# Attention with seven of seven block products: 49 of 64 in passes over 1024 queries

## The chip, the cores and the metric

The kernel runs on one core of a Trainium2 chip, in fp32. The core has TensorE (PE in the profile; PEld are its weight loads), VectorE (DVE), ScalarE (ACT), GpSimd (POOL) and SyncE (SP, which here issues DMAs), and 16 DMA engines. The metric is the device time of the whole program in microseconds. Three runs of the kernel before took 3640.42, 3641.31 and 3642.59 us; the median is 3641.31.

## The reference

The input has two images of 512 channels and 64 x 64 pixels. Two layers are added to it one after the other, each on a group-normalised copy. Layer 0 is a deformable convolution; the change leaves it alone. Layer 1 is attention over the 4096 pixels of an image, an output projection, a batch norm over both images and a relu:

```python
px = jnp.transpose(x.reshape(B, C, N), (0, 2, 1))
q = jnp.tanh(px @ Wq.T)            # 64 wide
k = jnp.tanh(px @ Wk.T)
v = px @ Wv.T
scores = jnp.einsum('bip,bjp,p->bij', q, k, align_w)
attn = jax.nn.softmax(scores, axis=2)
content = px + attn @ v
content = content @ Wfc.T + bfc
out = g * (c - mean) * jax.lax.rsqrt(var + BN_EPS) + b
return jax.nn.relu(out)
```

Scores are bounded by the sum of the absolute values of `align_w`, since the tanh is between -1 and 1. So no maximum is subtracted, and the sum of the exponentials divides at the end. Queries, keys and their product with `align_w` are 64 wide; values are 512 wide, so the product of the exponentials with the values is the large one: 4096 x 4096 x 512 for each image.

## The kernel before

**Shape of the program.** Layer 0 (lines up to 1236) leaves the sum of the input and its own output in DRAM (`x1_d`), [channel, pixel], in eight chunks of 512 pixels for each image. Then comes the attention, which has two stages for each image, and at the end the batch norm over both images. The order of the instructions in this part is the order of the code (`manual_schedule`); each engine runs its own queue in that order and waits for others through semaphores.

**Values.** Wv and Wfc have been multiplied beforehand (`wc_d`), so the attention's value product gives the output projection at once. For each of four groups of 1024 pixels, `pk` (L1439) makes keys and queries with a tanh; then `values` (L1371 to L1400) makes values for four pairs of 128-pixel tiles. The product of each pair is itself made of seven block products in place of eight (a Strassen form of Winograd's kind): seven products of two matmuls into PSUM, one ACT copy (L1388) and eleven DVE operations (L1389 to L1399), and the result is stored to DRAM as the seven block combinations that the next stage wants (L1400). The sums of the pixels' blocks that the seven products need come from `sum_pixels` (L1279 to L1282), on DVE for the first group and on POOL for the others.

**Query blocks.** For each of eight blocks of 512 queries the kernel runs over 16 key pairs (256 keys) and two more steps with the output weights `w7`, which project the residual. In `produce` (two pairs ahead) PE makes the scores of a pair (L1345), ACT takes the exponential (L1349), and DVE forms the query side's block sums (L1352 to L1355) and adds to the total (L1362). Then PE multiplies with the values, which SP loads two pairs ahead. The matrix product is cut in 2 x 2 x 2 blocks, and seven block products take the place of eight. Six run side by side in the six PSUM banks (L1500), two matmuls each; the seventh runs in a pass of its own after the others (L1543) with the sums `t3` kept in SBUF and the seventh combination of the values loaded again. That makes 18 x 14 = 252 matmuls of 128x256 for each block. Near the end of the block PE adds the total over partitions and spreads it (`pr`, L1471), DVE scales the residual `xq` with it (L1472 to L1478) and takes the reciprocal (L1480). ACT and DVE evacuate the six banks (L1521 to L1526) while PE is in the seventh pass; `finish_chunk` adds the seventh product's part in the next block. Results of image 0 go to DRAM, those of image 1 stay in SBUF.

**Tail.** When both images are done, the batch statistics are made; for every chunk ACT applies scale, shift and relu, DVE adds the residual, and SP stores. Image 0's results and residuals are loaded back for it.

**Guard.** The attention runs on this fast path always. Behind it the core compares the sum of |align_w|, divided by `SCORE_MAX` (40, L527), with one, and two other bounds with their limits; only where one is passed does a general path run as well. For these inputs the sum of |align_w| is 3.83.

Of the kernel before, what the change touches and what calls it, by code (L numbers as in the profile page):

```python
# [2 lines left out]

# [14 lines left out]
P = 128  # L18
# [508 lines left out]
SCORE_MAX = 40.0  # L527
# [43 lines left out]
def window_path(ctx: ExitStack, tc: tile.TileContext, t_in: dict, out: bass.AP, far: bass.AP, sums: bass.AP):  # L571
# [8 lines left out]
    c0_d = dram.tile([NCH, P, KB, CH], F32, name="wc0")  # L580
    wc_d = dram.tile([P, KB, C], F32, name="wvfc")
    v_d = [[dram.tile([P, 7, C // 2], F32, name=f"wv{n}_{k}") for k in range(S // P // 2)] for n in range(NB)]
# [653 lines left out]
    with ExitStack() as l1, tc.manual_schedule():  # L1236
        cp = l1.enter_context(tc.tile_pool(name="w1c", bufs=NCH, reuse_waits="tile"))
        bnp = l1.enter_context(tc.tile_pool(name="w1bnp", bufs=1))
        bst = bnp.tile([P, KB, NB * NCH, 6], F32, name="bst")
        last, res = [], []  # L1240
        HC = C // 2
        HQ = CH // 2
        NPAIR = S // P // 2

        with ExitStack() as at, ExitStack() as inner:
            aw = at.enter_context(tc.tile_pool(name="w1w", bufs=1))
            wk = at.enter_context(tc.tile_pool(name="w1work", bufs=2))
            iw = l1.enter_context(tc.tile_pool(name="w1in", bufs=1, side="right", reuse_waits="tile"))
            vw = inner.enter_context(tc.tile_pool(name="w1v", bufs=3, side="right"))
            vv = inner.enter_context(tc.tile_pool(name="w1vv", bufs=3, side="right"))  # L1250
            ps = at.enter_context(tc.tile_pool(name="w1ps", bufs=1, space=PSUM))

            def bank(i, name):
                return ps.tile([P, CH], F32, tag=f"A{i}", name=name)

            class Bank:


                def tile(self, shape, dtype, tag, name):
                    return ps.tile(shape, dtype, tag="A5", name=name)  # L1260

            pixels = {}
            ones = iw.tile([P, P], F32, name="ones_k")
            nc.vector.memset(ones, 1.0)

            def chunk(n, ch, queue):
                t = cp.tile([P, KB, CH], F32, tag="c", name="xt")
                queue.dma_start(t, x1_d[n][ch])
                return t

            def load_pixels(n, i):

                pair = [chunk(n, 2 * i + h, nc.scalar if n or i == 0 else nc.sync) for h in range(2)]
                return pair, [cp.tile([P, 2, 2, CH], F32, tag="c", name=name) for name in ("xsa", "xsb")]

            def sum_pixels(engine, pair, sums):

                (a1, a2), (sa, sb) = [x.rearrange("p (j r) q -> p j r q", j=2) for x in pair], sums
                engine.tensor_add(sa[:, 0], a2[:, 0], a2[:, 1])  # L1279
                engine.tensor_sub(sa[:, 1], sa[:, 0], a1[:, 0])  # L1280
                engine.tensor_sub(sb[:, 0], a1[:, 0], a2[:, 0])
                engine.tensor_sub(sb[:, 1], a1[:, 1], sa[:, 1])  # L1282

            def value_output():
                t = wk.tile([P, KB, C], F32, tag="x", name="wc", bufs=1)
                nc.sync.dma_start(t, wc_d)
                return t

            def sum_value_output(wc):

                t = wk.tile([P, 2, 4, HC], F32, tag="tx", name="wcs", bufs=1)
                b = wc.rearrange("p (j r) (l c) -> p j r l c", j=2, l=2)
                nc.vector.tensor_sub(t[:, :, 0, :], b[:, 0, :, 1, :], b[:, 0, :, 0, :])
                nc.vector.tensor_sub(t[:, :, 1, :], b[:, 1, :, 1, :], t[:, :, 0, :])
                nc.vector.tensor_sub(t[:, :, 2, :], b[:, 1, :, 1, :], b[:, 0, :, 1, :])
                nc.vector.tensor_sub(t[:, :, 3, :], t[:, :, 1, :], b[:, 1, :, 0, :])
                return t

            def normalize(t, sc, bi):
                for kb in range(KB):  # L1300
                    nc.scalar.activation(
                        t[:, kb, :], t[:, kb, :], AF.Identity, bias=bi[:, kb : kb + 1], scale=sc[:, kb : kb + 1]
                    )

            pixels[0] = load_pixels(0, 0)
            wc = value_output()
            pixels[1] = load_pixels(0, 1)
# [11 lines left out]
            w7 = aw.tile([P, 2, 7, HC], F32, name="w7")  # L1319
            bfc = load("L1_conv_bfc", [P, KB], None, aw)  # L1320
            gamma = load("L1_conv_gamma", [P, KB], None, bnp)
            beta = load("L1_conv_beta", [P, KB], None, bnp)
            for x in pixels[0][0]:
                normalize(x, *norms[0])
            sum_pixels(nc.vector, *pixels[0])
            wcs = sum_value_output(wc)

            kq = iw.tile([P, NCH, CH], F32, name="kq")
            qs, tots, made, vs, v7s = {}, {}, {}, {}, {}

            def queries(qb):

                rows = slice(DQ * (1 - qb % 2), DQ * (2 - qb % 2))
                nc.vector.tensor_scalar(kq[rows, qb, :], kq[rows, qb, :], al[rows], None, ALU.mult)
                q = vw.tile([P, CH], F32, name="q", bufs=2)
                for h in range(2):
                    nc.vector.tensor_copy(q[h * DQ : (h + 1) * DQ, :], kq[rows, qb, :])
                qs[qb] = q

            def produce(qb, kp):  # L1340

                pS = ps.tile([P, 2, CH], F32, tag="st", name="pS")
                for h in range(2):
                    c0, r = (kp % 4) * P, slice(h * DQ, (h + 1) * DQ)
                    nc.tensor.matmul(  # L1345
                        pS[:, h, :], kq[r, 2 * (kp // 4) + h, c0 : c0 + P], qs[qb][r, :], start=True, stop=True
                    )
                e = vw.tile([P, 4, HQ], F32, name="e")
                nc.scalar.activation(e.rearrange("p a q -> p (a q)"), pS.rearrange("p h q -> p (h q)"), AF.Exp)  # L1349
                tt = vw.tile([P, 3, HQ], F32, name="tt")  # L1350
                t3 = wk.tile([P, HQ], F32, name="t3", bufs=NPAIR + 2)
                nc.vector.tensor_sub(t3, e[:, 3, :], e[:, 1, :])  # L1352
                nc.vector.tensor_add(tt[:, 0, :], t3, e[:, 0, :])
                nc.vector.tensor_sub(tt[:, 2, :], tt[:, 0, :], e[:, 2, :])
                nc.vector.tensor_sub(tt[:, 1, :], e[:, 1, :], e[:, 0, :])  # L1355
                e2 = e.rearrange("p (h a) q -> p h (a q)", h=2)
                if kp == 0:
                    tots[qb] = vw.tile([P, CH], F32, name="tot", bufs=2)
                    nc.vector.tensor_add(tots[qb], e2[:, 0, :], e2[:, 1, :])
                else:  # L1360
                    for h in range(2):
                        nc.vector.tensor_add(tots[qb], tots[qb], e2[:, h, :])  # L1362
                made[qb, kp] = e, tt, t3

            def operands(b, tt):
                return (b(0), b(2), tt[:, 0, :], tt[:, 1, :], b(3), tt[:, 2, :])
# [305 lines left out]
```

## Time and profile before

The profiled execution has a span of 3638.9 us; the median of the timed runs is 2.4 us above it. The attention layer takes the last 2423 us.

| stretch of the span (us) | what runs | length | PE busy | DVE busy | DMA GB/s |
|---|---|---|---|---|---|
| 1216.2 to 1351.9 | values, image 0 | 135.7 | 131.1 | 103.6 | 173 |
| 1351.9 to 2386.2 | eight query blocks, image 0 | 1034.3 | 1034.3 | 522.5 | 134 |
| 2386.2 to 2516.7 | values, image 1 | 130.5 | 129.0 | 102.4 | 154 |
| 2516.7 to 3552.5 | eight query blocks, image 1 | 1035.8 | 1034.7 | 518.7 | 132 |
| 3552.5 to 3638.9 | batch norm, relu, stores | 86.4 | 0.6 | 43.9 | 373 |

A line of the windows gives a stretch, its length, and for each engine the busy time with the number of instructions, in the order PE, PEld, DVE, ACT, POOL; behind them the TensorE clock that was granted (1.00 is full), the share of time in which the DMA engines were busy, and GB/s. Each fp32 matmul is two instructions for PE. A line of a timeline gives start, duration, engine, line, operation, out<-in, shape and count; in brackets is how long the engine had been idle and who released it. A line of the groups gives busy time and mean ns of one behind the bar.

### The profile page before, as it was taken

What the parts mean: (1) busy time and instruction counts of PE and PEld (TensorE: products, weight loads), DVE (VectorE), ACT (ScalarE), POOL (GpSimd) and SP (SyncE); (2) the same over time, 40 slices, a digit from 0 to 9 for tenths busy, and PEclk for the clock granted to TensorE, in tenths of its full rate; (3) what the DMA queues carried; (4) which work ended last, traced back from release to release, by engine and by line L of the source; (5) the groups of instructions that cost most, each with busy time, mean ns of one, the idle gap of its engine ahead of it and who ended that gap; (6) DMA issues with size and microseconds to landing.
All of it is one profiled execution on the core that took longest, in us unless ns stands there. A gap on an engine that the chain in (4) does not pass through costs nothing.

```text
span 3638.9 us, 38933 instructions
## 1 busy us (share of the span) xinstructions
PE 3408.9 (94%) x15155; PEld 2428.8 (67%) x15155; DVE 2358.5 (65%) x3549; ACT 1306.8 (36%) x1693; POOL 284.7 (8%) x190
## 2 busy tenths in 40 slices
PE   5789999999998999999999999999999999999990
PEld 2355555555555677777777777777777777777770
DVE  8899999999996674554555455476455545545544
ACT  2577778878876321111211111121111111111115
POOL 1121121121120110000000000031000000000000
PEclk9899999999999999999999999999999999999995
DMA  6334334334323444333433433444333343333359
GB/s 213 98 114 139 125 94 127 119 94 128 114 84 111 169 169 152 125 125 126 142 124 113 156 124 102 143 182 176 125 130 113 104 153 111 113 132 124 113 186 376
DMA packets 173941, 497.31 MB, mean 137 GB/s; under 512 B 21520, under 2 KB 55056, under 8 KB 164272
## 3 DMA queue, kind: packets, MB, share of 16 engines
q1 hardware_dynamic: 165360, 460.09, 37.4%
q10 hardware_dynamic: 8352, 34.61, 2.6%
q8 instruction: 121, 1.98, 0.2%
q14 instruction: 76, 0.62, 0.0%
q0 software_dynamic: 32, 0.00, 0.0%
HBM read 403.34 MB, written 91.29 MB: 136 GB/s over the span
## 4 chain that ended last, share of the span: by engine, by line
PE 77%; DVE 15%; DMA 3%; ACT 2%; issue 1%; POOL 1%; SPq 0%; ACTq 0%; DVEq 0%; POOLq 0%
PE acc L1500 42%; DVE conv L814 10%; PE pS L1345 7%; PE p L1543 6%; PE py L998 6%; PE pq L783 5%; PE pa L978 5%; PE pv L1385 3%; PE pk L1439 1%; PE p_mean L830 1%; DMA early<-in_x 1%; DVE o L876 1%; DMA in_w<-in_L_conv_in_w 1%; DMA out<-ct 0%; DVE v L1399 0%
## 5 line engine op out<-in xcount | busy, mean ns | idle before, releaser
L1500 PE MATMUL acc<-e,v 128*128 128x256 f32 x3072 | 768.2, 386 | 0.0
L1349 ACT ACTIVATE e<-pS 128x1024 f32<-128x1024 f32 x256 | 262.2, 1024 | 1386.3 <-PE pS L1345 1317.9
L1500 PE MATMUL acc<-tt,v 128*128 128x256 f32 x3072 | 748.2, 380 | 0.2 <-DVE v L1396 0.2
L1500 PEld LDWEIGHTS acc<-e,v 128*128 128x128 f32 x3072 | 566.5, 190 | 233.2 <-issue 165.4
L1500 PEld LDWEIGHTS acc<-tt,v 128*128 128x128 f32 x3072 | 582.4, 190 | 91.0 <-issue 10.6
L1352 DVE TENSOR_TENSOR t<-e 128x256 f32<-128x256 f32 x256 | 108.9, 425 | 761.0 <-ACT e L1349 761.0
L814 DVE SCALAR_TENSOR_TENSOR conv<-xn,L_conv_dw_w_sb,conv 128x504 f32<-128x504 f32 (+1 forms) x512 | 409.4, 808 | 37.6 <-ACT conv L808 23.8
L1362 DVE TENSOR_TENSOR tot<-tot,e 128x512 f32<-128x512 f32 x480 | 330.3, 688 | 8.3
L1345 PE MATMUL pS<-q,kq 64*128 64x512 f32 x1024 | 289.0, 641 | 0.0
L978 PEld LDWEIGHTS pa<-bt,patch 96*128 96x128 f32 x2048 | 249.6, 196 | 57.0 <-issue 33.5
L978 PE MATMUL pa<-bt,patch 96*128 96x128 f32 x2048 | 253.6, 281 | 7.1 <-ACT bt L964 5.5
L964 ACT COPY bt<-pb 96x1024 f32<-96x1024 f32 x124 | 234.6, 2007 | 57.6 <-PE pb L959 55.3
L783 PE MATMUL pq<-in_w,xn 128*128 128x512 f32 x512 | 240.4, 613 | 6.6 <-DVE o L876 4.5
L998 PE MATMUL py<-dT,L_conv_out_w_sb 128*128 128x512 f32 x512 | 236.1, 605 | 4.8 <-ACT dT L989 4.8
L1543 PE MATMUL p<-t,v 128*128 128x256 f32 x1024 | 231.4, 382 | 1.1 <-DMA v<-wv 1.1
L1543 PEld LDWEIGHTS p<-t,v 128*128 128x128 f32 x1024 | 192.1, 190 | 47.8 <-issue 21.2
L871 PE MATMUL po<-om_w_pg,feat 128*128 128x432 f32 x512 | 203.7, 543 | 2.5 <-ACT feat L854 2.5
L989 ACT COPY dT<-pa 32x256 f32<-32x256 f32 x496 | 180.0, 363 | 65.7 <-PE pa L978 56.3
L998 PEld LDWEIGHTS py<-dT,L_conv_out_w_sb 128*128 128x128 f32 x512 | 97.5, 194 | 123.2 <-issue 112.6
L783 PEld LDWEIGHTS pq<-in_w,xn 128*128 128x128 f32 x512 | 95.3, 197 | 114.5 <-issue 98.7
L871 PEld LDWEIGHTS po<-om_w_pg,feat 128*128 128x128 f32 x512 | 93.7, 192 | 94.5 <-issue 89.2
L1345 PEld LDWEIGHTS pS<-q,kq 64*128 64x128 f32 x1024 | 77.1, 184 | 84.9 <-issue 84.9
(210 smaller groups left out, 3713.2 us busy)
## 6 DMA issues: line engine op xcount, KB each, us to landing
v<-wv SPq DMA_DIRECT2D x252, 768.0 KB
patch<-xt SPq DMA_DIRECT2D x256, 192.0 KB
v<-wv SPq DMA_DIRECT2D x256, 128.0 KB
wv<-v SPq DMA_DIRECT2D x32, 896.0 KB
xt<-xj SPq DMA_DIRECT2D x128, 128.0 KB
res<-in_x SPq DMA_DIRECT2D x64, 256.0 KB
wx<-res SPq DMA_DIRECT2D x64, 256.0 KB
xq<-wx SPq DMA_DIRECT2D x16, 1024.0 KB
```

The lines of the kernel that those rows point to most:

```text
L783: nc.tensor.matmul(pq, xn[:, kb, 1 + 2 * t : 3 + 2 * t, :].rearrange("p r c -> p (r c)"), in_w[:, kb, :], start=(kb == 0), stop=(kb == KB ...
L814: nc.vector.scalar_tensor_tensor(dst, src, wt, dst, ALU.mult, ALU.add)
L871: nc.tensor.matmul(po[:, : 3 * GP], f[:, kb, t * P : (t + 1) * P], om_w[:, kb].rearrange("p a k g -> p (a k g)"), start=(kb == 0), stop=(k ...
L964: copy(bt[:SN].rearrange("s g q d -> s d (g q)")[:, d0 : d0 + 4, :], pb[:SN])
L978: nc.tensor.matmul(pa[:, p], xp[:SN, p, cb * P : (cb + 1) * P], bt[:SN, 4 * cb : 4 * cb + 4, PX * s + p, :], start=True, stop=True,)
L989: copy(dst, src)
L998: nc.tensor.matmul(py, out_w[:, kb, cb * P : (cb + 1) * P], dT[:, kb, :], start=(kb == 0), stop=(kb == KB - 1))
L1345: nc.tensor.matmul(pS[:, h, :], kq[r, 2 * (kp // 4) + h, c0 : c0 + P], qs[qb][r, :], start=True, stop=True)
L1349: nc.scalar.activation(e.rearrange("p a q -> p (a q)"), pS.rearrange("p h q -> p (h q)"), AF.Exp)
L1362: nc.vector.tensor_add(tots[qb], tots[qb], e2[:, h, :])
L1500: nc.tensor.matmul(acc[j][:, cb * HQ : (cb + 1) * HQ], v[:, j, cb * P : (cb + 1) * P], ops[j], start=(kp + cb == 0), stop=(kp + cb == NPAI ...
L1543: nc.tensor.matmul(p7[:, cb * HQ : (cb + 1) * HQ], v7[:, cb * P : (cb + 1) * P], t3, start=(k + cb == 0), stop=(k + cb == NPAIR + 2),)
```

## The change

The product of the exponentials with the values is cut in 4 x 4 x 4 blocks, 64 of them, and the seven-of-eight form is used at both levels, so that 49 products remain. The outer level is run as seven passes, one after the other, over all keys; the inner level is run inside each slot of a pass.

- A chunk has 1024 queries (two of the old blocks). Its 63 slots are seven passes of nine: eight groups of 512 keys and one group for the output weights. A slot is seven matmuls of 128x256 (L1478 of the new file), so a chunk has 441. They add up in two PSUM tiles `accx` and `accy`, from a pool of three.
- The scores are made once for each chunk, 32 pairs in 32 events with slots given by the table `EVENTS`: 'e0' and 'e2' mostly in slots that belong to the chunk before, 'e3' in slots 5 to 12, 'e1' in slots 13 to 20. The exponentials of a whole chunk stay in SBUF. `settle`, one event later, turns them into the outer level's combinations in place: a total and a transform for e0 and e2, a transform for e3; for e1 also a second row made of e0, e1 and e3 and the total of the chunk's second half.
- The inner sums of a slot (`inner_sums`, L1457 and L1458) are made by DVE four slots ahead (`LEAD`), in five buffers. The values of a slot are loaded by SP three slots ahead (448 KB).
- `spread_total`, the sum over partitions of a total on PE (L1434), stands in slot 5 for the first half's total and in slot 22 for the second's, ahead of the slot's products; ACT copies it and `scale_residual` uses it. The total's last adds (`total`, L1428 and L1430) stand in slots 4 and 21. The reciprocals stand in slots 7 and 25.
- At the end of a pass `first_copy` and `collect` evacuate the two tiles, and the passes' results are added to four output pieces in turn.
- In the values stage each pair of tiles still takes seven products of two matmuls, but into PSUM tiles of the same pool of three; the evacuation is one ACT copy and five DVE operations (L1639 to L1644), and `forms` (L1332 to L1345) makes the two levels' combinations on DVE for each pair of pairs and stores them, 7 x 448 KB. Twelve score events of the image's first chunk are also in this stage. The output weights go through `forms` too, in image 0. Queries go through DRAM (`q_d`).
- All large tiles come from one ring of 36 pieces of 4 KB per partition (`w1ring`), so that a tile waits until the piece 36 tiles before it is done with.
- Results go to DRAM except for the last chunk's. The tail's loads begin at slot 47 of the last chunk, in pieces of 512 KB.
- `SCORE_MAX` goes from 40 to 6.

```diff
-SCORE_MAX = 40.0
+NG = S // P // 4
+SLOTS = 7 * (NG + 1)
+LEAD = 4
+SCORE_MAX = 6.0
...
-                            for cb in range(2):
-                                nc.tensor.matmul(
-                                    acc[j][:, cb * HQ : (cb + 1) * HQ], v[:, j, cb * P : (cb + 1) * P], ops[j],
-                                    start=(kp + cb == 0), stop=(kp + cb == NPAIR + 2),
-                                )
...
+        ring = l1.enter_context(tc.tile_pool(name="w1ring", bufs=36, reuse_waits="tile"))
...
+            def forms(raw, store):
+
+                for j in (0, 3, 1, 5):
+                    nc.vector.tensor_add(raw[j][:, 1, :], raw[j][:, 1, :], raw[j][:, 3, :])
+                yield
+
+                def finish(j):
+                    t = raw.pop(j)
+                    nc.vector.tensor_sub(t[:, 4, :], t[:, 0, :], t[:, 1, :])
+                    nc.vector.tensor_add(t[:, 5:7, :], t[:, 4, :].unsqueeze(1).to_broadcast([P, 2, P]), t[:, 2:4, :])
+                    nc.sync.dma_start(store[j], t[:, :7, :])
+
+                def combine(j, a, b):
+                    raw[j] = piece("vform", (P, 8, P))
+                    nc.vector.tensor_sub(raw[j][:, :4, :], raw[a][:, :4, :], raw[b][:, :4, :])
...
+            def transform(t):
+                x = blocks(t)
+                nc.vector.tensor_sub(x[:, 1], x[:, 1], x[:, 0])
...
+            def second_row(c, g):
+                t0, t1 = c.e["e0", g], c.e["e1", g]
+                nc.vector.tensor_sub(t0, t1, t0)
+                nc.vector.tensor_add(t1, t1, c.e["e3", g])
+                if g < NG:
+                    add_total(c, 1, t1)
+
+            def settle(c, key, g):
+
+                e = c.e[key, g]
+                if key in ("e0", "e2"):
+                    add_total(c, 0, e)
+                transform(e)
+                if key == "e1":
+                    second_row(c, g)
+
+            def total(c, qh):
+                t = c.tot[qh]
+                nc.vector.tensor_add(t[:, 1, :], t[:, 1, :], t[:, 0, :])
+                if qh:
+                    nc.vector.tensor_add(t[:, 1, HQ:], t[:, 1, HQ:], t[:, 0, :HQ])
+
+            def spread_total(c, qh):
+                p = pair_bank("pr")[:, 0, :]
+                nc.tensor.matmul(p, ones, c.tot.pop(qh)[:, 1, :], start=True, stop=True)
+                nc.scalar.copy(rin[:, qh, :], p)
...
+            def inner_sums(c, p, g):
+                x = blocks(c.e[ORDER[p][0], g])
+                t = wk.tile([P, 3, HQ], F32, name="tt", bufs=LEAD + 1)
+                nc.vector.tensor_sub(t[:, 0], x[:, 1], x[:, 3])
+                nc.vector.tensor_add(t[:, 1:3], t[:, 0].unsqueeze(1).to_broadcast([P, 2, HQ]), x[:, 0:3:2])
+                return t
...
+            EVENTS = {}
+            for g, l in enumerate((-14, -13, -11, -10, -9, -7, -6, -5)):
+                EVENTS.setdefault(l, []).append(("e0", g))
+            for g in range(NG):
+                EVENTS.setdefault(g - 4, []).append(("e2", g))
+                EVENTS.setdefault(5 + g, []).append(("e3", g))
+                EVENTS.setdefault(13 + g, []).append(("e1", g))
...
+                def slot(self, s):
+                    k, l = divmod(s, SLOTS)
+                    c = self.chunks[k]
+                    nxt = self.chunks[k + 1] if k + 1 < NCH // 2 else None
+                    self.fetch(s + 3)
+                    if l % (NG + 1) == 0 and self.ends:
+                        next(self.ends[-1], None)
+                    self.before(l, c)
...
+                    self.at(l, c, s)
+                    if l + LEAD not in (8, 26):
+                        self.sums(s + LEAD)
+                    if l in (4, 21):
+                        total(c, int(l > 4))
+                    p, g = divmod(l, NG + 1)
+                    products(c, p, g, self.v.pop(s), self.t.pop(s))
```

## The prediction

> **What bounds the kernel now.** I read the page's busy shares, the chain of waits, and then a table of windows, because the change touches only the attention layer, the last two thirds of the span.
>
> ```profile
> PE 3408.9 (94%) x15155; PEld 2428.8 (67%) x15155; DVE 2358.5 (65%) x3549; ACT 1306.8 (36%) x1693; POOL 284.7 (8%) x190
> ...
> PE 77%; DVE 15%; DMA 3%; ACT 2%; issue 1%; POOL 1%; SPq 0%; ACTq 0%; DVEq 0%; POOLq 0%
> ```
>
> PE carries most of the chain. The windows cut the attention layer into values of image 0, its eight query blocks, the same two for image 1, and the tail:
>
> ```profile
> core 0: us, PE busy (x) PEld busy (x) DVE busy (x) ACT busy (x) POOL busy (x), PEclk, DMA share, GB/s
> 1216.20:1351.90 135.70, 131.14 (x528) 99.20 (x529) 103.64 (x211) 35.01 (x57) 29.50 (x12) 0.99 0.45 173
> 1351.90:2386.20 1034.30, 1034.28 (x4549) 796.52 (x4550) 522.46 (x920) 171.80 (x190) 5.17 (x3) 1.00 0.40 134
> 2386.20:2516.70 130.50, 128.97 (x526) 97.53 (x524) 102.44 (x198) 29.33 (x50) 34.65 (x14) 1.00 0.40 154
> 2516.70:3552.50 1035.80, 1034.67 (x4548) 796.16 (x4548) 518.68 (x920) 167.43 (x183) 0.00 (x0) 1.00 0.38 132
> 3552.50:3638.90 86.40, 0.56 (x4) 0.16 (x3) 43.91 (x37) 45.73 (x65) 0.50 (x2) 0.52 0.95 373
> ```
>
> In the two long windows PE is never idle and its clock is full; DVE is half used (522 of 1034). In the values windows DVE stands at 104 of 136 and 102 of 131, much nearer. The tail is DMA at 0.95 of its engines. So PE work removed from the query blocks is worth its full time only while DVE keeps up, and work added to DVE in the values stage has little room.
>
> **Prices.** PE, from the timeline of one query block: twelve products of 128x256 follow each other in 2.59 us (row below: 2.75 with the drain of the last, next row starting 2.59 later), two instructions for each fp32 product, so 0.4317 us per product. A key pair's period is 6.43 us for 12 products; the remaining 1.25 is its score pair. DVE durations come from the rows:
>
> ```profile
> 1584.40 2.75 PE L1500 MATMUL acc<-tx,w 128*128 128x256 f32 x12
> 1586.99 1.24 PE L1500 MATMUL acc<-xq,w 128*128 128x256 f32 x5
> ```
> ```profile
> L1362 DVE TENSOR_TENSOR tot<-tot,e 128x512 f32<-128x512 f32 x480 | 330.3, 688 | 8.3
> L1352 DVE TENSOR_TENSOR t<-e 128x256 f32<-128x256 f32 x256 | 108.9, 425 | 761.0 <-ACT e L1349 761.0
> L1480 DVE RECIPROCAL rin<-pr 128x512 f32<-128x512 f32 x16 | 53.6, 3350 | 0.0
> ```
> ```profile
> 1216.77 1.21 DVE L1279 TENSOR_TENSOR xsa<-xt 128x1024 f32<-128x1024 f32 x1
> 1218.02 1.23 DVE L1280 TENSOR_TENSOR xsa<-xsa,xt 128x1024 f32<-128x1024 f32 x1
> ```
>
> So DVE pays 0.42, 0.69 and 1.22 us for 256, 512 and 1024 columns; dependent neighbours are spaced 0.47 and 1.25, independent ones 0.34, 0.61 and 1.14.
>
> **PE in the query blocks.** One block of before, from a window of its own:
>
> ```profile
> 1565.38:1695.12 129.74, 129.74 (x571) 99.63 (x571) 65.91 (x117) 21.01 (x23) 0.00 (x0) 1.00 0.39 130
> ```
>
> Two blocks (1024 queries) take 2 x 129.7 = 259.5 us: 504 products, 32 score pairs, two sums over partitions (0.86 each). After, one chunk has 63 slots of seven products: 441 x 0.4317 = 190.4, 32 score pairs 40.0, two sums 1.7; together 232.1, which is 27.4 less. The first twelve score pairs of each image (eight of e0, four of e2) come before its first slot, so 12 x 1.25 = 15 us of PE move into the values stage. Undisturbed, an image's attention would be 4 x 192.1 + 116 x 1.25 = 913 plus about 2 at its end, against 1034: minus 119.
>
> **DVE in the query blocks, and the stall.** Counted in the new program's order, one chunk gives DVE 107 operations of 256 columns, 86 of 512, 74 of 1024, two copies, eight bn_stats and two reciprocals: 44.9 + 59.3 + 90.3 + 1.4 + 5.5 + 6.7 = 208 us, against 2 x 65.9 = 132 now. That is 90% of PE's 232, so the mean fits; the question is where it bunches. It does in slots 13 to 21, where the scores called e1 arrive. Each is settled (L1417) with a transform (256), two operations of the second row (1024) and a total (1024): 0.47 + 1.25 + 1.25 + 1.14 = 4.1, and the slot's inner sums (256 and 512) make it 5.2 us. PE needs seven products and a score pair, 4.27. DVE starts about 2.4 us late (score to exp to DVE, as in the trace: 1.23 to the exp, 1.02 in it). Slot by slot it ends at 7.05 in slot 14, 22.6 in 17, 30.4 in 18 (which also evacuates the pass that has ended, 2.6), 36.7 and 43.1 in 19 and 20 (each with an add of a pass, 1.14), and 49.5 in 21 with the total's last adds. PE, unhindered, stands at slot 22 after 8 x 4.27 + 3.02 = 37.2. There its next instruction is the sum over partitions of that total (L1434), and all products of slot 22 are queued behind it. So PE waits about **12.3 us in each of eight chunks**. Bounds: 9, if independent operations keep a pitch of 0.34 and 0.61 throughout; 16, if the ring's pieces, which the last three e1 exps get only when PE has done with them (about 1.1 each), add to it. I take the middle walk, because its operations do depend on each other.
>
> After the wait PE starts at a lower clock. The trace shows this once in the values stage, where DVE shut out by POOL let PE idle 2.79 us:
>
> ```profile
> 1239.86 2.59 POOL L1279 TENSOR_TENSOR xsa<-xt 128x1024 f32<-128x1024 f32 x1 [107.60 <-ACT xt L1301]
> ...
> 1242.65 2.57 DVE L1398 TENSOR_TENSOR v<-v,u 128x256 f32<-128x256 f32 x1
> ...
> 1248.09 1.26 PE L1385 MATMUL pv<-wc,xsb 128*128 128x256 f32 x4 [2.79 <-DVE v L1389]
> ...
> 1249.14 1.91 PE L1385 MATMUL pv<-wcs,xsb 128*128 128x256 f32 x4
> ```
>
> Four products took 1.91 where they take 1.03; some 1.5 us was lost. I add 1.5 per stall (0 to 3). The page "TensorE: Matmul & The Clock Gate", section "What's actually happening", halves the clock only after an idle window of about 3.4 us; the row did so after 2.79. By the page the loss could be up to 3.4 us of half speed, 1.7 lost, so 1.6 us more over eight stalls, which changes nothing.
>
> Other waits on PE (slot 5's first sum, the pass boundaries with three accumulator tiles) come to at most 0.3 us each by the same walk, and the two reciprocals stand where PE has work for four slots; cost zero while the inner sums keep their lead of four slots (otherwise 3.35 each). One image's attention is then 913 + 4 x 13.8 + 2 = 970: **64 less than now, twice**.
>
> **Values stage.** PE: 16 tiles, 96.7; keys and queries 27.5; twelve score pairs 15: 139. DVE: 16 evacuations of 2.5 (three of 256, two of 512), 40; block sums (L1332), per pair of tiles four of 512, seven of 256 and eleven of 128 columns, the last not in the trace: between half a 256 operation and a whole one, taken as 0.29 from the line through 0.42 and 0.69: 8.6 to 9, times 8 = 69; twelve settles of 1.64, 20; first sums 4. Three blocks of POOL sums lie beside it: the rows above show a 256 operation with both inputs in SBUF at 2.5 us while POOL works, and one such block costs DVE about 6.4 us, so 19. DVE begins about 10 us into the stage. That is 162 to 164 us. The page "SBUF — State Buffer", section "Who interferes with whom", says the same of DVE operations with two SBUF inputs, and would let the block sums, all of that kind, wait as often as they meet a POOL operation; it speaks against this change, whose DVE work there is mostly such. If each POOL operation met one, the price would be 12 x 2.1 = 25 in place of 19. Then the first load of v stands on SP's queue behind the last store of block sums, which DVE ends; its landing costs 3 to 4. Image 1: 166 against 130.5, **plus 36**. Image 0 also forms the output weights' blocks, 8.6 more, and the second normalisation: 178 against 135.7, **plus 42**. Bounds for the two: plus 40 in all if DVE's part overlaps PE better (PE's 139 plus start and load) and plus 120 if POOL costs double.
>
> **Tail.** From slot 47 of the last chunk prefetches are issued. Some 14 MB of them and 7.3 MB of v must pass in 48 us, 441 GB/s, where the tail shows 373: PE waits for v some 5 (0 to 10). Behind PE's end the remaining bytes take about 89 against 86.4. **Plus 8** (0 to 12).
>
> **Sum.** -128 + 78 + 8 = -42 on the profiled span of 3638.9, so 3597 less a little; that execution lies 2.4 below the median 3641.3, which goes back on. I predict **3597 us** (3638.9 - 44 + 2.4).
>
> **Rivals.**
> *DVE catches up and the total is ready* (chance 0.10). The inner pitch of 0.34/0.61 in the rows speaks for it, the dependence of each settle's operations against. Without the stall: 3597 - 8 x 13.8 = 3487.
> *The e1 slots take longer, slower than before* (0.25). The total comes later by each e1 exp's wait for a ring piece: if all eight wait 1.1 us and DVE waits with them, a stall grows by 8.8, 70 us in all: 3667. The gain is gone from 5.5 us more per chunk (44 / 8), that is 0.6 us in each of nine slots. For it: 36 pieces hold 32 score tiles of a chunk and much else. Against: only three of eight exps wait in the order that I followed.
> *The change doesn't do what it says* (0.05): if the guard on scores sent these inputs down the general path, or the stall and the values stage took just the 219 us of products back. The sum of the absolute align weights, which bounds a score, is 3.83 here, under 6 as under 40, so only the second remains: 3641.
>
> **How the numbers follow.** The likeliest (0.60) is 3597, with its own range 3550 to 3635 from the stall's 9 to 16 and the stage's bounds. To leave out no more than 2 in 10 the range goes up to the slower rival, 3667, and down half way to the faster, 3530. About 0.2%, 7 us, is what a measurement of this kernel can tell. Faster 0.70 (the likeliest, less its upper edge, and the faster rival), same 0.05, slower 0.25.
>
> **What would show it.** In the changed kernel's waits: PE before the sum at L1434, released by DVE's total (L1428 or L1430), eight times about 12 us with the clock below full behind it. In windows: a values stage of 166 to 178 with DVE above 90% and PE waiting for it; chunks of about 246; 3528 products at two instructions each and 0.216 us. The prediction is wrong if the stall at L1434 is under 5 us or over 18, if PE waits for exps or for v in every slot, or if DVE's operations of 1024 columns take more than 1.25.

## The result and the profile after

The changed kernel takes 3677.22 us (median of four runs, 3674.86 to 3680.62) against 3640.86 us of the kernel before, measured beside it. The ratio is 1.0102, 95% interval 1.0088 to 1.0116: slower by one per cent, where 3597 us and faster had been forecast. The profiled execution has a span of 3673.1 us, 4.1 below the median.

The page's busy shares and chain of the changed kernel:

```profile
PE 3239.0 (88%) x14147; PEld 2261.1 (62%) x14147; DVE 2969.6 (81%) x4107; ACT 1362.9 (37%) x1802; POOL 272.5 (7%) x186
...
PE 63%; DVE 27%; DMA 4%; ACT 3%; issue 1%; POOL 1%; SPq 0%; ACTq 0%; DVEq 0%; POOLq 0%
```

PE lost 170 us of work and DVE won 611, and DVE's share of the chain went from 15% to 27%. The windows, cut at the same places of the program as before (columns as there):

```profile
1216.20:1436.40 220.20, 156.50 (x570) 108.03 (x569) 162.27 (x334) 61.24 (x89) 28.54 (x12) 0.84 0.52 196
1436.40:2413.90 977.50, 925.89 (x4004) 704.92 (x4005) 775.03 (x1083) 177.58 (x217) 0.00 (x0) 0.97 0.43 138
2413.90:2594.40 180.50, 149.62 (x565) 105.38 (x564) 148.45 (x297) 52.26 (x79) 28.55 (x12) 0.90 0.54 199
2594.40:3575.90 981.50, 927.29 (x4004) 704.28 (x4004) 769.33 (x1077) 171.73 (x209) 0.00 (x0) 0.98 0.44 148
3575.90:3673.10 97.20, 0.56 (x3) 0.19 (x3) 48.13 (x55) 48.89 (x68) 0.50 (x2) 0.51 0.92 346
```

| stage | before | forecast | after | after minus forecast |
|---|---|---|---|---|
| values, image 0 | 135.7 | 178 | 220.2 | +42.2 |
| attention, image 0 | 1034.3 | 970 | 977.5 | +7.5 |
| values, image 1 | 130.5 | 166 | 180.5 | +14.5 |
| attention, image 1, and tail | 1122.2 | 1064.4 | 1078.7 | +14.3 |

The last column adds up to 78.5, which is the whole miss in spans (3673.1 against 3594.6). The attention came within 1.2 per cent of the forecast (977.5 and 981.5 against 970): it became 57 and 54 us shorter. More than half of the miss is in one place, the values stage of image 0; both values stages together cost 134.5 us more than before, against 78.

In the attention the foreseen stall is there. The timeline of one chunk, DVE's last operations of the e1 slots and PE's sum behind them:

```profile
1542.22 0.68 DVE L1428 TENSOR_TENSOR tot<-tot 128x512 f32<-128x512 f32 x1
1542.94 0.42 DVE L1430 TENSOR_TENSOR tot<-tot 128x256 f32<-128x256 f32 x1
...
1543.52 2.05 PE L1434 MATMUL pr<-tot,ones_k 128*128 128x512 f32 x2 [10.31 <-DVE tot L1430]
1545.36 1.91 PE L1478 MATMUL accx<-e,v 128*128 128x256 f32 x4
```

PE had been idle for 10.31 us and then ran at half its clock: from this sum to the start of the second slot behind it takes 5.87 us where 0.96 + 3.02 are usual, 1.9 lost. All eight chunks show the same (see below).

The values stage of image 0 looks different from the forecast. DVE is busy for 162 of its 220 us, and PE for 157 at a mean clock of 0.84; both are idle a good part of the time. The waits of the whole program on PE and, in this stage, on DVE (for whom, us in total, times, longest):

```profile
PE pr L1434 <- DVE tot L1430: 82.5, 8, 10.3
PE pvy L1633 <- DVE u L1641: 33.6, 6, 14.1
...
PE accx L1478 <- DMA v<-wv: 15.3, 5, 13.1
PE accx L1478 <- DVE tt L1457: 10.5, 1, 10.5
PE pS L1396 <- DVE gn_var L627: 9.7, 1, 9.7
...
PE pk L1700 <- DVE gn_gm L618: 6.1, 1, 6.1
```
```profile
DVE vform L1640 <- ACT u L1639: 32.5, 5, 14.1
DVE u L1642 <- PE pvy L1633: 11.0, 5, 3.4
DVE xs L1307 <- ACT xt L1290: 8.8, 1, 8.8
```

The two engines wait for each other in turn. PE stops for DVE (33.6 us in both stages, and 9.7 and 6.1 for the second norm), mostly goes on at half its clock, and then DVE waits 32.5 us for the first copy of the next tile. A stretch of the timeline shows three of the causes at work:

```profile
1286.16 7.37 DVE L1332 TENSOR_TENSOR vform<-vform 128x128 f32<-128x128 f32 x4
...
1300.74 0.89 DVE L1332 TENSOR_TENSOR vform<-vform 128x128 f32<-128x128 f32 x4
...
1306.73 2.04 PE L1633 MATMUL pvy<-wc,xs 128*128 128x256 f32 x4 [14.06 <-DVE u L1641]
...
1318.94 0.16 DVE L618 COPY gn_gm<-gn_p 128x8 f32<-128x8 f32 x1
...
1319.16 8.59 PE L1700 MATMUL pk<-xt,early 128*128 128x512 f32 x16 [6.08 <-DVE gn_gm L618]
```

Four small block sums take 7.37 us beside POOL (its `sum_pixels` runs from 1283.89 to 1293.39) and 0.89 without it. A series of block sums, the output weights' among them, keeps DVE from the next tile until 1306, and PE waits 14.06. The norm's tiny product sits in the one score tile, its reader of 0.16 us stands on DVE behind another series, and PE's keys and queries, which need the tile, wait 6.08 and then take 8.59 in place of 7.03.

### The profile page after: what moved, and what is told of

It is laid out like the page before. It is cut to its first block, busy times and chain, and to the rows that moved or that the text cites. A ratio compares the mean times of both kernels' runs of the same rounds, so it can differ in the third digit from the quotient of the medians.

```text
span 3673.1 us, 37956 instructions
## 1 busy us (share of the span) xinstructions
PE 3239.0 (88%) x14147; PEld 2261.1 (62%) x14147; DVE 2969.6 (81%) x4107; ACT 1362.9 (37%) x1802; POOL 272.5 (7%) x186
## 4 chain that ended last, share of the span: by engine, by line
PE 63%; DVE 27%; DMA 4%; ACT 3%; issue 1%; POOL 1%; SPq 0%; ACTq 0%; DVEq 0%; POOLq 0%
PE accy L1478 20%; PE accx L1478 16%; DVE conv L820 9%; PE py L1004 6%; PE pS L1396 5%; PE pq L789 5%; PE pa L984 5%; DVE tot L1405 2%; DVE e L1412 2%; DVE e L1413 2%; PE pvy L1633 2%; PE pk L1700 1%; DVE tt L1458 1%; DVE vform L1332 1%; PE pvx L1633 1%
## 5 line engine op out<-in xcount | busy, mean ns | idle before, releaser
L1478 PE MATMUL accy<-tt,v 128*128 128x256 f32 x2016 | 602.2, 380 | 0.0
L1478 PE MATMUL accx<-e,v 128*128 128x256 f32 x1792 | 489.1, 396 | 25.8 <-DMA v<-wv 15.3
L1478 PEld LDWEIGHTS accx<-e,v 128*128 128x128 f32 x1792 | 329.5, 193 | 226.4 <-issue 153.1
L1478 PE MATMUL accy<-e,v 128*128 128x256 f32 x1792 | 461.7, 380 | 0.0
L1478 PEld LDWEIGHTS accy<-tt,v 128*128 128x128 f32 x2016 | 385.0, 191 | 53.0
L1478 PEld LDWEIGHTS accy<-e,v 128*128 128x128 f32 x1792 | 342.5, 191 | 47.3
L1396 PE MATMUL pS<-q,keys 64*128 64x512 f32 x1024 | 294.7, 653 | 35.1 <-ACT e L1400 25.5
L1458 DVE TENSOR_TENSOR tt<-tt,e 128x512 f32<-128x512 f32 x448 | 310.0, 692 | 15.3
L1478 PE MATMUL accx<-tt,v 128*128 128x256 f32 x1008 | 302.8, 382 | 0.0
L1457 DVE TENSOR_TENSOR tt<-e 128x256 f32<-128x256 f32 x448 | 187.6, 419 | 140.9 <-PE accy L1478 139.8
L1405 DVE TENSOR_TENSOR tot<-tot,e 128x1024 f32<-128x1024 f32 x176 | 214.9, 1221 | 29.1 <-ACT e L1400 27.1
L1478 PEld LDWEIGHTS accx<-tt,v 128*128 128x128 f32 x1008 | 193.8, 192 | 27.1
```

The lines of the kernel that those rows point to most:

```text
L1396: nc.tensor.matmul(p[:, a, :], keys[r, i, (2 * u + h) * P : (2 * u + h + 1) * P], c.q[r, qh, :], start=True, stop=True)
L1405: nc.vector.tensor_add(c.tot[qh], c.tot[qh], t)
L1457: nc.vector.tensor_sub(t[:, 0], x[:, 1], x[:, 3])
L1458: nc.vector.tensor_add(t[:, 1:3], t[:, 0].unsqueeze(1).to_broadcast([P, 2, HQ]), x[:, 0:3:2])
L1478: nc.tensor.matmul(out, v[:, blk, :], op, start=(first and g == 0), stop=(final and g == NG))
```

## The experiments

The question was what the stages are made of: the stall in the attention (bunched work, or DVE as the bound), and in the values stage DVE's amount of work against the order in which PE and DVE wait for each other. Lengths of stages are of the profiled executions, cut as in the table above; changes of the whole time are between medians. The values stage of image 0 is counted from 1216.2 in every run, although the last product of layer 0, which no run changes, ends anywhere from 1210.5 to 1218.1. Where a few us matter, the length from that product is given as well; in the changed kernel it is 219.9 (before: 136.6).

**The stall: scores of e3 and e1 in turn.**

```diff
-                EVENTS.setdefault(5 + g, []).append(("e3", g))
-                EVENTS.setdefault(13 + g, []).append(("e1", g))
+                EVENTS.setdefault(5 + 2 * g, []).append(("e3", g))
+                EVENTS.setdefault(6 + 2 * g, []).append(("e1", g))
```

> The scores of e3 and e1 alternate over slots 5 to 20, in place of eight slots of e3 and then eight of e1; nothing else is changed. Theory (the stall is DVE's work bunched in the e1 slots): a pair of slots then asks DVE for 0.47 + 4.1 + 2 x 1.08 = 6.7 us against 8.5 of PE, so DVE keeps up, and PE's wait before the second sum over partitions (L1434) falls from 10.3 us to 1 to 4 us, with the lower clock behind it gone. A chunk goes from 247.6 to about 238, the whole by 60 to 80 us, to about 3605. Rival one (DVE is the bound over the whole chunk, its 208 us and its gaps together): the wait goes to other slots and the chunk stays above 244; the whole falls by under 25. Rival two (the ring of 36 pieces): earlier e1 tiles find no free piece, PE waits before scores in place of the sum, and the time is the same within 15.

Measured: 3630.14 us, ratio to the kernel before 0.997 (0.9959 to 0.9982), 47 below the changed kernel. The same wait of PE, of this kernel:

```profile
1539.52 2.05 PE L1434 MATMUL pr<-tot,ones_k 128*128 128x512 f32 x2 [4.16 <-DVE tot L1430]
```

It fell from 10.31 to 4.16 but no further, and the half clock stayed. The attention of an image fell from 977.5 to 955.4, a chunk by 5.5. The gain of 47 lies between theory and first rival. That it is there at all, with the amount of work on DVE unchanged, speaks for the bunching; it is smaller than expected because DVE's total is still 4 us late. The second rival falls: no new wait before scores appeared. The next run takes the rest away.

**The stall: the sum one slot later.** The kernel of the last run, and:

```diff
-                    if l in (5, 22):
+                    if l in (5, 23):
```

> Scores of e3 and e1 alternate as before, and the second sum over partitions with the scaling of the residual moves from slot 22 to slot 23. Theory (what is left of the stall, 4.2 us, is DVE's last settle and total, which end one slot after PE asks): three more us of PE's work stand ahead of the sum, the wait falls to about 1 us and no lower clock follows; a chunk goes from 242.1 to 236 to 238, the whole by 30 to 45 against the alternating kernel, to about 3590. Rival (DVE is the bound, the wait moves to slot 26, whose inner sums need the scaled residual, or to the ring): under 12.

Measured: 3602.43 us, ratio 0.9899 (0.9883 to 0.9916), 28 below the last. The attention of image 0 is 941.4 us, 36 below the changed kernel's, 9 for each chunk. PE's waits in this kernel:

```profile
PE accy L1478 <- DVE ct L1508: 16.9, 8, 2.1
...
PE pr L1434 <- DVE tot L1430: 9.1, 8, 1.1
```

The stall of 82.5 us is down to 9.1. In its place stands a new one of 2.1 in each chunk: the third pass's evacuation is late on DVE. The gain is just under the theory's range, short by this wait.

**The norm out of the values stage.**

```diff
-                        for _ in range({5: 1, 7: 2, 11: 2, 12: 1}.get(4 * i + t, 0) if n == 0 else 0):
-                            next(later, None)
...
                     at.slot(s)
+                    if n == 0 and s in (94, 96, 98, 100, 102, 104):
+                        next(later, None)
```

> The steps of the second image's group norm leave the values stage of image 0 and are made in the second chunk of its attention, in slots where no scores are made. Theory (in the values stage PE and DVE wait for each other in turn, because a short PE result in the one score tile has to be read by DVE behind a series of block sums): the two waits of PE, 6.1 before pk and 9.7 before a score pair, go, with the half clock behind each; the stage goes from 220 to 200 to 207 us and the whole falls by about 15 (13 to 20). Rival (DVE's amount of work sets the stage and the waits only change their place): the stage stays above 215 and the whole falls by under 5.

Measured: 3654.46 us, 22.8 below the changed kernel; the stage of image 0 went from 220.2 to 202.1 (from layer 0's last product: 219.9 to 200.6), the others stayed within 1.2 us. Among the norm's steps are six DVE operations of less than 0.2 us each; with the PE products and the ACT step between them they cost 19 us by where they stood. The theory holds; the gain of the whole is a little above its 13 to 20.

**The output weights' block sums earlier.**

```diff
-                    if i == 1:
+                    if i == 0:
                         load_w = {}
```

> The output weights' block sums are made with the first group of pixels in place of the second. Theory (the burst): PE's wait of 14.1 us in the second group, in which DVE does the weights' block sums and those of a pair in one series, falls to about 5, as at the other groups; the first group has room for 8.6 us of DVE, because DVE waits there some 10 us in all. The whole falls by 6 to 12. Rival (the same work on the same engine costs the same wherever it is): the same within 4.

Measured: 3674.69 us, 2.5 below; the stage is 216.9 (from layer 0's last product 217.6, 2.3 less). In the second group PE's wait fell from 14.06 to 5.80, as the theory said. But in the first group, where the sums now stand, it grew from 4.87 to 9.05, and the norm's wait behind them from 6.08 to 7.05. The time did not follow: the rival holds. The work stands elsewhere on the same engine, and there was no room for it in the first group.

**The first loads and sums ahead of the last block sums.**

```diff
+                for s in range(3):
+                    at.fetch(s)
+                for done in at.open:
+                    settle(*done)
+                at.open = []
+                for s in range(LEAD):
+                    at.sums(s)
                 for g in pending:
                     for _ in g:
                         pass
-                for done in at.open:
-                    settle(*done)
-                at.open = []
-                for s in range(3):
-                    at.fetch(s)
-                for s in range(LEAD):
-                    at.sums(s)
```

> At the end of each values stage the first three loads of v are issued, the open scores settled and the first four inner sums made ahead of the last block sums, in place of behind them. Theory (the attention's first product waits for the order of the queues, not for the data): PE's waits of 13.1 and 10.5 us before its first product fall by some 6 to 10 each; the whole falls by 12 to 20. Rival (the loads land late because the block sums' stores fill the DMA engines): the waits stay above 9 us and the whole falls by under 6.

Measured: 3655.78 us, 21.4 below. PE's waits before the attention's first product fell from 13.05 to 3.24 and from 10.53 to 5.51, the stages from 220.2 to 209.3 and from 180.5 to 172.5. It was the order of the queues; in image 1 the wait fell by 5, a little less than the theory's 6 to 10.

**The block sums left out.**

```diff
-                    nc.vector.tensor_sub(t[:, 4, :], t[:, 0, :], t[:, 1, :])
-                    nc.vector.tensor_add(t[:, 5:7, :], t[:, 4, :].unsqueeze(1).to_broadcast([P, 2, P]), t[:, 2:4, :])
+                    nc.gpsimd.memset(t[:, 4:7, :], 0.0)
...
-                    nc.vector.tensor_sub(raw[j][:, :4, :], raw[a][:, :4, :], raw[b][:, :4, :])
+                    nc.gpsimd.memset(raw[j][:, :4, :], 0.0)
...
-                nc.vector.tensor_sub(raw[3][:, :4, :], raw[3][:, :4, :], raw[5][:, :4, :])
```

> Left out: all arithmetic of the block sums in the values stage and of the output weights' (L1332 to L1345); GpSimd writes zeros where they would stand, and the stores stay. It prices DVE's block sums. Theory (they set the stage, by their own work, by what they meet of POOL, and by the waits in turn with PE): DVE loses 69 + 9 us of work and some 17 of collisions in the two stages' length; both stages come down to PE's 139 us plus start, last loads and the norm's steps: image 0 from 220 to about 165 to 175, image 1 from 180 to about 148 to 155; the whole by 75 to 95 against the changed kernel, to about 3590. Rival (PE's products with three accumulator tiles, or the loads at the end, set the stage whatever DVE does): under 40.

Measured: 3604.43 us, 73 below, just under the range; the stages are 170.5 and 153.9 (from 220.2 and 180.5), and PE waits nowhere for an evacuation. Counted from layer 0's last product, image 0's stage is 173.2. So the block sums, with what they bring with them, are worth 47 and 27 us. What is left is still 37 and 23 above the kernel before: some 15 of that are the twelve score pairs that now stand in the stage (1.25 each).

**The second pair's block sums in one series behind the fourth tile.**

```diff
-                            for _ in range(4):
+                            for _ in range(8 if t == 3 and i < 3 else 4):
                                 next(pending[0], None)
```

> The block sums of a group's second pair of tiles are made whole behind its fourth tile, in place of half there and half behind the next group's first tile; they then lie beside PE's keys and queries (7 us), where DVE has nothing to do now (waits of 4.4 and 1.8 us in image 1's stage at each group). Theory (waits in turn): the stages lose 3 to 8 us each, the whole 6 to 15. Rival (DVE's work of the stage is the same and only its place changes): the same within 4.

Measured: 3692.62 us, 15 above the changed kernel, where a gain was expected: the theory's sign was wrong here. The stages became 234.9 and 184.9. The waits of PE in this kernel:

```profile
PE pvy L1633 <- DVE u L1641: 41.4, 9, 14.0
...
PE pS L1396 <- DVE gn_var L627: 11.9, 1, 11.9
...
PE pk L1700 <- DVE gn_gm L618: 10.0, 1, 10.0
```

A longer series ahead of the next tile's evacuation makes three more waits of PE, and those for the norm grow from 6.1 and 9.7 to 10.0 and 11.9. The same work in the same stage costs more the longer DVE's series is; that DVE has a gap beside the keys and queries did not help.

**The combination, with and without that series.** The first is the alternating scores, slot 23, the norm, the weights, the early loads and the series together; the second leaves the series out.

> The alternating scores, the sum in slot 23, the norm's steps out of the stage, the weights' block sums with the first group, the early loads and the block sums behind the fourth tile, all together. If the causes are apart, their gains add up: 47 + 38 + 22 + 21 + 2 + 10 = 140 below the changed kernel, about 3537, some 100 below the kernel before. If they share one cause (DVE's work in the stage, or the bytes of the end), it stays above 3570.

> The combination of before without the block sums behind the fourth tile, whose run alone had cost 15 us. If the remaining gains add up (75 from the alternating scores and slot 23, 22 from the norm's steps, 21 from the early loads, 2 from the weights), the time is about 3556, some 17 under the combination with it and 84 under the kernel before. Rival (in the combination the waits that the block sums behind the fourth tile lengthen are gone, the norm's above all, so that they cost nothing there): the same as the other combination within 5, about 3573.

Measured: 3572.76 and 3564.89 us, ratios 0.9804 (0.9787 to 0.9821) and 0.9789 (0.9775 to 0.9804). The second's stages are 183.5 and 172.5 against 196.2 and 177.8 with the series, so the series costs 13 and 5 us without the norm too (in image 0 11.5 from layer 0's last product on). The first lies above 3570, where its rival had put it, but through the series, not through a cause that the others share: with the series at the 15 us that it had cost alone, the single changes add up to 106 and 3571, and 3572.76 was measured. Neither expectation for the second was met: the medians differ by 8, between 5 and 17, and its gains nearly add up (112 measured, 121 as a sum).

**The pixels' sums on DVE.**

```diff
-                                psums[i + 1] = sum_pixels(nc.gpsimd, pixels[i + 1])
+                                psums[i + 1] = sum_pixels(nc.vector, pixels[i + 1])
```

In the second combination, and then alone in the changed kernel:

> As the last, and the pixels' block sums of groups two to four are made by DVE in place of POOL. Theory (a POOL series of four costs DVE 5.8 us of collisions; made on DVE it is 4 x 1.22 = 4.9 us): the gain is about 1 us for each of six series, so the time is the same within 6 us. Rival (the collisions cost more, because the lengthened DVE operations hold up PE's products and its clock falls): faster by 10 to 25.

> The changed kernel with the pixels' block sums of groups two to four made by DVE in place of POOL; nothing else. It prices POOL's collisions by themselves. In the combination this took 19 us off. Theory (DVE's operations with both inputs in SBUF are held while POOL works, and PE, with three accumulator tiles, is held behind them): 10 to 20 us less than the changed kernel's 3677. Rival (the gain comes from the combination alone, where the norm's waits no longer cover it): under 6.

Measured: 3545.68 us, ratio 0.9745 (0.9731 to 0.9758), 19 below the second combination; and alone 3660.43 us, 16.8 below the changed kernel. In the first of the two the rival was right, and the theory of the second run took that up. PE's waits for the evacuation of value tiles fell from 28.7 to 17.8 us in the combination and from 33.6 to 22.3 alone. A group of the changed kernel in the first 184 us of image 0's stage, and the same of the combination with DVE's sums:

```profile
L1332 DVE TENSOR_TENSOR vform<-vform 128x128 f32<-128x128 f32 x32 | 22.6, 767 | 0.0
```
```profile
L1332 DVE TENSOR_TENSOR vform<-vform 128x128 f32<-128x128 f32 x36 | 8.0, 283 | 0.0
```

Without POOL an operation takes 283 ns, with it 767 in the mean. DVE takes over 3 x 4.9 = 14.7 us of work in each image and the stages still get shorter: alone 220.2 to 215.7 (from layer 0's last product 219.9 to 217.7) and 180.5 to 172.5. That is 10 of the 16.8; the two profiled executions are 10.8 apart, and the rest of the difference between the medians is not placed.

**The second reciprocal later.** The fastest kernel so far, and:

```diff
-                    if l in (7, 25):
+                    if l in (7, 29):
```

> The fastest combination, with the second reciprocal of a chunk (3.35 us on DVE) moved from slot 25 to slot 29. In the combination PE waits 2.1 us in each of eight chunks for the first evacuating add of the third pass, which DVE does behind that reciprocal and two inner sums. Theory: those waits (16.9 in all) go, and the time falls by 12 to 18 to about 3531. Rival (DVE is late by its total amount there, and the wait moves on to the next pass): under 5.

Measured: 3526.09 us (3524.11 to 3529.3), ratio 0.9687 (0.9674 to 0.9700): 3.1% faster than the kernel before, and 151 us below the changed kernel. The waits of 2.1 us for the third pass's evacuation are gone, and the attention of an image is 932.4 and 935.0 us (945.1 and 944.8 in the combination). The gain of 19.6 is a little above the theory's 12 to 18: behind two of the eight waits the clock had been halved for 3.4 us, too. So the reciprocal was not covered where it stood.

## Why the prediction was wrong

**The products.** Right. (What the forecast calls twelve products in 2.59 us are twelve instructions, six products; its 0.4317 us for each is right.) 441 products in a chunk at the old pace: a slot takes 3.02 us, with a score pair 4.27, as forecast. An image's attention came to 977.5 and 981.5 against 970.

**The stall before the second sum.** Right in its place, cause and nearly its size: 10.3 us in each of eight chunks against 12.3, and 1.9 for the half clock against 1.5. The runs with alternating scores and slot 23 show that it is bunching, not DVE's whole amount of work.

**Other waits on PE in the attention.** Too small: "at most 0.3 us each" was 1.12 before slot 5's sum and 0.73 twice before scores, in every chunk, in all 2.6 us a chunk. That is 10.3 us an image, and the first slot, at the half clock that the end of the values stage leaves, lost 2.7 more; the smaller stall gave back 4 x 1.6 = 6.4. The difference, 6.6, is nearly the 7.5 of image 0. That the two reciprocals cost nothing held as long as the stall covered the second one; with the stall gone it cost 2.1 us a chunk.

**The values stage: the step that failed.** The forecast added up DVE's work (152 us in image 1, 161 in image 0) and let DVE work without a gap from its first operation to the last load. The work was right: DVE was busy for 148.5 and 162.3 us. The gaps were not 10 us at the start and 4 at the end but 32 and 58 in all. So the sign that the forecast gave, DVE above 90% there, did not come (82% and 74%), while none of its signs of being wrong came either. In the sum of one engine's durations there is no place for two engines that wait for each other in turn: DVE's series of block sums hold up the evacuation, PE has room for one and a half tiles only, stops, mostly comes back at half its clock, and then DVE runs dry. The runs put numbers on the parts. In image 0, from layer 0's last product on: 19 us by the place of the norm's small operations, which the forecast had named only in passing; 10 by the order of the first loads and sums behind the last block sums, forecast as 3 to 4; 2 by POOL's making of the pixels' sums; 2 by the weights' series. In image 1, where 14.5 were missed, the order is worth 8 and POOL 8. These are each measured alone and overlap in part; what is left of the 42 is not separated further, and no run gave PE more room. Leaving the block sums out took 47 and 27 us off the stages, where the forecast's 78 and 69 us of them had DVE as the only bound.

**POOL.** The price of 6.4 us for a series was right for DVE. The rows of L1332 (767 against 283 ns, 32 times) and of L1345 (1199 against 692 ns, 8 times) give 19.5 us over three series, 6.5 each, not the 5.8 of the expectation above. What came on top was waits of PE. The rule that the forecast cited from the Trainium skill, "SBUF — State Buffer", section "Who interferes with whom", gave the right sign: block sums with both inputs in SBUF are what POOL held up, here with 7.37 against 0.89 us for four. The evacuating operations beside the same POOL series, with one input in PSUM (L1642 to L1644), kept their 0.69 and 0.41 us.

**Tail.** 97.3 us after PE's end against 89 forecast; waits for v were 2, not 5. The first relu comes 9.7 us after PE's end (7.2 before), and DMA falls to 247 GB/s in the ten us from 3586 on (before: 315 in the ten us from 3562 on). No run took this apart; the cause is left open.

**The rivals.** The time lies beyond the slower rival's 3667, but not by its mechanism: the e1 slots were, if anything, a little faster than forecast. The case that happened, a values stage that costs far more than the sum of its work, was not among the rivals; its upper bound of plus 120 for both stages was passed at 134.5, and it had been put down to POOL.

## What to carry to other kernels

A stage in which two engines hand tiles to each other through few buffers is not priced by the busier one's sum of work. Ask instead how long the longest series on the one engine is, compared with the lead that the buffers give the other, and add to each idle time that lowers the clock what the half pace costs (here 1.9 us behind a wait of 10.3). Before a change gives a half-used engine new work, look for the small operations that another engine waits for (a norm's copy, the first loads, a total) and keep them out of the long series: here six moves of order and one change of engine, with the same arithmetic, turned one per cent slower into three per cent faster.

## What the runs showed of the hardware

The length of a wait alone did not decide whether the clock fell. In the changed kernel four products after an idle time of 2.36 us took 1.10 us, after 2.56 us 2.05. In the combination with DVE's sums PE waits 2.11 us for the same add in each of eight chunks; two of them:

```profile
1510.49 0.70 PE L1478 MATMUL accy<-tt,v 128*128 128x256 f32 x2 [2.11 <-DVE ct L1508]
...
1749.34 1.22 PE L1478 MATMUL accy<-tt,v 128*128 128x256 f32 x2 [2.11 <-DVE ct L1508]
```

Behind the second the granted clock is 0.50 for 3.4 us, behind the first it is 1.00. Of the eight, two were followed by the half clock and six were not; a wait of 3.18 us in the values stage of the same kernel (at 1297.17) was not either. Nor need it be one long wait. At the end of the changed kernel's first values stage short score products alternate with waits of about 1.1 us, and in the middle of them the pace halves:

```profile
1415.76 1.13 PE L1396 MATMUL pS<-q,keys 64*128 64x512 f32 x4 [1.12 <-ACT e L1400]
1418.01 2.08 PE L1396 MATMUL pS<-q,keys 64*128 64x512 f32 x4 [1.12 <-ACT e L1400]
```

What goes with this in the traces is a fixed grid: from the values stage to PE's end, every stretch of half clock in the changed kernel lasted 3.41 us or a multiple of it (6.83, 10.24, 13.65 and so on). In the 3.4 us before a fall PE was busy in part: for 0.99 us before 2523.6, for about 1.5 before 1417.7. The idle time of 2.36 us had fallen across two such stretches (PE busy for 1.48 of 3.3 us in the one, 2.86 in the other). So how a wait lies on the grid counted as well as its length. The Trainium skill, "TensorE: Matmul & The Clock Gate", section "What's actually happening", gives the lower clock after an idle window of about 3.4 us; the length agrees with the grid here, but the window before a fall was not wholly idle. After the wait of 14.06 us the half pace lasted about 5 us.

An addition of 128x128 took 0.284 us, as the line through 0.42 and 0.69 had given (0.29).
